# Two-layer sparse graph block on one core: hub slots fetched as runs of words, later record scatters, nine early gathers, two lists later

## The chip, the core and the metric

The kernel runs on one core of one Trainium2 chip. The metric is the device time in microseconds of one execution. A core has a matrix engine (TensorE, PE in the profile), three vector-like engines (VectorE or DVE, ScalarE or ACT, GpSimd or POOL), a sync engine (SP), and 16 DMA engines that move data between HBM and on-chip memory (SBUF). Each engine runs its own instruction queue in order; semaphores tie the queues together. PE writes into PSUM banks of 128 partitions x 512 words. Transfers that are issued by SP have fixed addresses; gathers and scatters by a list of row numbers are issued by POOL.

## The reference

x has 2708 rows of 1024 words; adj is a 2708 x 2708 matrix of zeros and ones, so sparse that a row has a handful of neighbours. All is float32. Two layers, each followed by a residual and a layer norm:

```python
q = x @ W_q.T + b_q;  k = x @ W_k.T + b_k;  v = x @ W_v.T + b_v
z = (q @ k.T) / sqrt(1024) * adj
z = where(z == 0, -10000, z)
x = layernorm(x + relu(softmax(z) @ v))          # layer 0: attention over neighbours
x = layernorm(x + adj @ (x @ weight) + bias)     # layer 1: sum over neighbours
```

## The kernel before

The kernel does not form the 2708 x 2708 scores. It uses the sparsity: M = W_q.T W_k once, y = x M, and the score of row n and neighbour m is the dot product of row n of y with row m of x. The attention output is the softmax-weighted sum r of the neighbours' rows of x, then turned by W_v.T. Rows without neighbours get the mean of all x. Rows are handled in 22 blocks of 128, sorted by degree so that each block has a fixed number of neighbour slots, `SLOTS`. Blocks 0 to 7 (`FAMILY` = 8) form the first family, blocks 8 to 21 the second; each family is sorted for itself.

**The stages, in order of time.**

1. The weights are loaded and transposed (to about 30 us).
2. M is computed on PE (`product_of_m`, to about 131 us). Behind its products DVE makes the neighbour lists: `list_columns` searches the six column ranges of one block of adj with `max_index` (L236) and leaves up to 24 column numbers per row in `keys`; `count_columns` lets ACT count the ones and loads the next block of adj. `EARLY` lists are spread over the products of M; the rest are put between the products of the y pairs by the table `between`. After list 9 the first family is sorted (`sort_begin(0)`, `sort_end(0)`).
3. y of blocks 0 to 7, in four pairs by a product scheme with fewer multiplications (`y_pair`, `pair_products`, L299); PE does them between 131 and 244 us. ACT or DVE empties the banks (`add`, L319 and L321). Behind the first pair the first family's records (neighbour numbers, row, degree; 28 words per row) are scattered into `tab_d` in sorted order and loaded back as `tabs`. `deal_hub` is a generator; each `next(deal)` emits its next part.
4. y of blocks 8 to 19, 21 and 20 one at a time (`y_block`, L379; `y_last`, L430; 244 to 466 us), each 32 matmuls of 512 columns. Beside each block the jobs of attention run: for the blocks 6, 5, 4, 3, 2, 2, 1, 1, hub, hub, 0, 0, 0 (blocks with many slots come in pieces of `PIECE` = 6). A job copies the constant y_bc into a tile on ACT (L472, L474), lets POOL add the gathered row of y onto it (`yg` or `xr`, L463), gathers one row of x per slot (`g`, L479, nine tiles in turn, `G1`), scores them on DVE (L1006), makes the softmax, and sums them on DVE (L1063, L1140) into `r`.
5. The attention products of block pairs and the first norm (466 to 756 us).
6. The second layer (756 to 1083 us): gathers of the normed rows, sums, products, norm.

**The hub.** The 32 rows of the highest degrees (`HUB`) have more neighbours than a record holds. Their rows of adj are cut into four quarters (`G` = 4), one per partition, and each quarter's neighbours (up to `HUB_KEYS` = 80) are drawn on DVE and stored as a list of `KW` = 96 words in DRAM, `keys_d`; the 16 words behind the 80 are zeros. The lists of all quarters lie behind one another. `place` holds at which dealt slot each list begins. The neighbours are dealt to 128 partitions of `HUB_SLOTS` = 11 slots each; a hub row gets as many partitions as it needs, and `row` says which hub row a partition works for. In the kernel before, the address of each slot is worked out on its own: eleven rows of DVE over all 128 lists (`at`, L592), and eleven gathers of one word per partition (`found`, in `gather_at`, L463), dealt out over four steps of the generator behind y blocks 11 to 14. From `found` come `valid_h` (L624), `less_h` and `tab_h`, the row numbers of the hub's gathers.

**What sets the order.** The queues are in order. POOL's queue holds the gathers, the scatters and a few table loads; a gather waits for its tile (its last reader on DVE) and for the landing of the POOL transfer eight before it. ACT's queue holds the bank copies and the copies of y_bc. The program order on each engine comes from a scheduler that takes instructions by priority; `tc.high_priority(URGENT)` puts an instruction ahead. `follow(later, earlier)` adds a wait by hand, most often for the last matmul of an earlier block, `products[-1]` or `products[-2]`, so that a queue doesn't stand still for something that is far off. In the main loop (L1363 to 1376) each y step runs `next(deal)`, `records_out` for the second family (two scatters a step into `tab_d`, L699, at blocks 10 to 16, and behind the last the load of the tables, L709), `records_back(1)` at block 19 (the copy into `degs`, L735, waits for block 18's products), and then the block's own products.

Pools give tiles their place in SBUF. A new tile on the place of a released pool waits for that pool's last users. `hub`, `work`, `g0` and `sums` are opened when the pools of the lists and y pairs (`lists`, `la`, `yb`) are released.

Of the kernel before, what the change touches and what calls it, by code (L numbers as in the profile page):

```python
# [9 lines left out]
F32 = mybir.dt.float32  # L10
BF16 = mybir.dt.bfloat16
I32 = mybir.dt.int32
# [4 lines left out]
ALU = mybir.AluOpType  # L17
# [4 lines left out]
P = 128  # L22
# [5 lines left out]
HUB_SLOTS = 11  # L28
HUB_KEYS = 80
FAMILY = 8  # L30

# [7 lines left out]
CLASSES = list(range(1, 14)) + [15, 17, 20, 24]  # L39
EARLY = 14  # L40
G1 = 9
# [40 lines left out]
def sparse_part(ctx, tc, x, xT, adj, wqT, wkT, wvT, bq, bk, bv, w1, b1, out):  # L82
# [28 lines left out]
    with es:  # L111
# [389 lines left out]
        def deal_hub():  # L501
# [39 lines left out]
            for i in range(0, HUB_KEYS, 8):  # L541
                nc.vector.max(keys[:, i:i + 8], a0)
                if i + 8 < HUB_KEYS:
# [41 lines left out]

            step = small("step", P)
            nc.vector.memset(step[:, 0:1], 0.0)
            nc.vector.scalar_tensor_tensor(step[:, 1:], place[:, :P - 1], float(KW), place[:, 1:], op0=ALU.add,
                                           op1=ALU.subtract)
            at = small("at", HUB_SLOTS)  # L590
            for j in range(HUB_SLOTS):
                nc.vector.scalar_tensor_tensor(junk, place, q[:, j:j + 1], step, op0=ALU.is_le, op1=ALU.mult,  # L592
                                               accum_out=at[:, j:j + 1])
            nc.vector.tensor_add(at, at, q)
            nc.vector.tensor_scalar_min(at, at, float(P * KW - 1))
            at_i = const.tile([P, HUB_SLOTS], I32, name="at_i")
            nc.vector.tensor_copy(at_i, at)

            row = small("row")
# [4 lines left out]
            nc.vector.tensor_copy(row_i, row)  # L604
            nc.vector.tensor_scalar(to_h, num, row, None, op0=ALU.is_equal)
            yield
            tr = p_tr.tile([P, 4, P], F32, name="tr")
# [11 lines left out]
            found = const.tile([P, HUB_SLOTS], F32, name="found")  # L619
            for j in range(HUB_SLOTS):  # L620
                gather_at(keys_d[:, :], at_i[:, j:j + 1], P, found[:, j:j + 1], behind=products[-1])
                if j % 3 == 2 or j == HUB_SLOTS - 1:
                    yield
            follow(nc.vector.tensor_scalar(valid_h, found, 0.0, None, op0=ALU.is_gt), products[-2])  # L624
            nc.vector.scalar_tensor_tensor(found, valid_h, -float(N + 1), found, op0=ALU.mult, op1=ALU.add)
# [218 lines left out]
        for b in range(0, FAMILY, 2):  # L844
            first = len(began)
            for k in range(min(3, NB - done)):
                if k:
                    between[first + 2 * k] = [lambda put: list_columns()]
                else:
                    list_columns()  # L850
                done += 1
                between[first + 2 * k + 1] = [count_columns]
            if b == 4:
                between[first + 4] = [lambda put: next(deal)]
            if b == 6:
# [20 lines left out]

        hp = es.enter_context(tc.tile_pool(name="hub", bufs=1, reuse_waits="tile"))
        wp = es.enter_context(tc.tile_pool(name="work", bufs=2, reuse_waits="tile"))
        gp = es.enter_context(tc.tile_pool(name="g0", bufs=G1, reuse_waits="tile"))
        rp = es.enter_context(tc.tile_pool(name="sums", bufs=RB, reuse_waits="tile"))  # L880
# [11 lines left out]
        def gather(src, b, word, n):  # L892
            return gather_slot(src, tabs[:n, b, word:word + 1], n, g_tile())

# [5 lines left out]
        def y_tile():  # L900

            filled[0] += 1
            if left_y and filled[0] % 4 in (3, 0):
                return wp.tile([P, D], F32, name="xr", bufs=2)
            return wp.tile([P, D], F32, name="yg")

# [162 lines left out]
        def r_tile(b):  # L1069

            if b in FIRST:
                return wp.tile([P, D], F32, name="r", tag="t")
            ring.append(b)
            return rp.tile([P, D], F32, name="r")
# [19 lines left out]
        def finish0(b, po, xr):  # L1094
            n = rows[b]
            t = (xb_pools[0] if b == last[-1] else wp).tile([P, D], F32, name="t", bufs=2)
            for h in range(NH):
# [90 lines left out]
        def project_pair(pair, A, S):  # L1188
            ts = [(xb_pools[0] if k else wp).tile([P, D], F32, name="t", bufs=2) for k in range(2)]
            bias = halves_of(bias_bc)  # L1190

            def whole(k, h, acc, what):
                add(halves_of(ts[k])[h], acc, what)

            pair_products(A, S, wv_q, wv_t, [bias, bias], [halves_of(t) for t in ts], whole, pair in (pairs[0], pairs[-1]))
            return ts
# [137 lines left out]
        for i, (kind, b) in enumerate(steps):  # L1334
# [29 lines left out]
            if kind == "y":  # L1364
                if FAMILY + 1 <= b < FAMILY + 7:
                    next(deal)
                if 2 <= b - FAMILY < 9:
                    records_out(*later_records, 2 * (b - FAMILY - 2), 2 * (b - FAMILY - 2) + 2, products[-2])
                if b == FAMILY + 11:
# [98 lines left out]
        def work1(unit, A, S, xrs):  # L1468

            ts = [wp.tile([P, D], F32, name="t", tag="t" if k % 2 == 0 else "yg") for k, _ in enumerate(unit)]  # L1470
            sums = [[stat.tile([P, 1], F32, name=f"sm{h}", bufs=6) for h in range(NH)] for _ in unit]
# [365 lines left out]
```

## Time and profile before

| what | us |
|---|---|
| six runs | 1089.21, 1091.35, 1085.18, 1079.99, 1079.20, 1075.07 |
| their median | 1082.58 |
| the profiled execution, its own time | 1084.41 |
| its span in the profile | 1082.7 |
| PE busy in the span | 963.5 (89%) |
| DVE busy | 834.7 (77%) |
| POOL busy | 562.1 (52%) |
| ACT busy | 410.2 (38%) |
| mean of one x gather on POOL (L479, 84 of them) | 1.341 |
| mean of one score on DVE (L1006) | 1.22 |
| one search of a list on DVE (L236, 132 of them), mean | 0.627 |
| granted clock of PE, mean | 0.957 |

How to read it: "us busy" of an engine is the time in which it executed; waits are the time in which an engine stood, put down to the instruction or transfer that ended the wait. `yo L319 <- PE` would mean a copy that waits for a product. Of a transfer the trace has the time of its issue on the engine's queue (what POOL is busy with) and the time when it lands. Line numbers are those of the kernel before, and in the changed kernel they are up to ten higher from the hub's part on. The windows by stage matter more than the sums, since the stages have different limits.

### The profile page before, as it was taken

How to read it: one execution, taken by the hardware profiler on the slowest of the kernel's cores; microseconds unless marked ns; L12 is line 12 of the kernel's file. 1: busy time of each engine (PE TensorE's matmuls, PEld its weight loads, DVE VectorE, ACT ScalarE, POOL GpSimd, SP SyncE). 2: the span in 40 equal slices, each digit the busy share in tenths (PEclk: the TensorE clock that was granted, in tenths of full speed). 3: DMA queues.
4: the chain of work that ended last, by engine and by line, in shares of the span. 5: the costliest groups of instructions: out<-in, count | busy, mean ns of one | idle time of the engine just before them, and what ended most of it. 6: DMA issues, size and time to landing. Idle time of an engine off the chain costs nothing.

```text
span 1082.7 us, 10444 instructions
## 1 busy us (share of the span) xinstructions
PE 963.5 (89%) x2697; PEld 450.9 (42%) x2697; DVE 834.7 (77%) x2045; ACT 410.2 (38%) x917; POOL 562.1 (52%) x454
## 2 busy tenths in 40 slices
PE   7999869999989589789999979897499999989894
PEld 6444324444434233335544434443244444435341
DVE  7999999926676778874999789677469877869632
ACT  4454445534433223414443434331312443351621
POOL 0441452305787574441766653554387777768420
PEclk9999899999999898899999999999699999999998
DMA  9567775648869766363468864669488789987741
GB/s 349 181 203 247 217 236 153 204 139 252 267 177 260 227 208 211 96 190 96 131 189 241 255 179 156 225 233 314 178 248 270 224 267 300 321 245 208 216 115 42
DMA packets 103293, 229.21 MB, mean 212 GB/s; under 512 B 19902, under 2 KB 47302, under 8 KB 103224
## 3 DMA queue, kind: packets, MB, share of 16 engines
q0 software_dynamic: 51376, 159.04, 48.3%
q1 hardware_dynamic: 51848, 69.41, 19.9%
q8 instruction: 23, 0.38, 0.1%
q14 instruction: 46, 0.38, 0.1%
HBM read 218.08 MB, written 33.64 MB: 232 GB/s over the span
## 4 chain that ended last, share of the span: by engine, by line
PE 23%; DVE 22%; issue 21%; DMA 17%; POOL 13%; ACT 1%; SPq 1%; POOLq 0%; another core or an unknown queue 0%; DVEq 0%; ACTq 0%
PE po L299 18%; POOL g L479 5%; DVE at_a L236 5%; DMA g<-in_x_dram,tabs 4%; DVE junkv L1006 3%; DVE r L1063 3%; DMA xr<-x_d,tabs 3%; PE po L379 2%; DMA yg<-y_d,tabs 2%; POOL xr L463 2%; POOL g L463 2%; DMA g<-x_d,tabs 1%; DMA wq_i<-in_wqT_dram 1%; DVE t L321 1%; DMA g<-in_x_dram,tab_h 1%
## 5 line engine op out<-in xcount | busy, mean ns | idle before, releaser
L379 PE MATMUL po<-m,xt 128*128 128x512 f32 x416 | 187.6, 612 | 22.2 <-ACT yo L319 22.2
L299 PE MATMUL po<-t,s_all 128*128 128x512 f32 x320 | 147.1, 603 | 14.9 <-DVE t L321 6.9
L479 POOL DMA_INDIRECT g<-in_x_dram,tabs x84 | 112.7, 1341 | 44.6 <-issue 17.7
L379 PEld LDWEIGHTS po<-m,xt 128*128 128x128 f32 x416 | 80.8, 196 | 126.6 <-issue 98.9
L1006 DVE SCALAR_TENSOR_TENSOR junkv<-yg,g 128x1024 uint8<-128x1024 f32 x69 | 84.2, 1221 | 41.3 <-DMA g<-in_x_dram,tabs 25.7
L1438 DVE SCALAR_TENSOR_TENSOR r<-g,valid,r 128x1024 f32<-128x1024 f32 x77 | 98.1, 1280 | 15.4 <-DMA g<-x_d,tabs 10.5
L299 PEld LDWEIGHTS po<-t,s_all 128*128 128x128 f32 x320 | 60.1, 192 | 97.4 <-issue 71.2
L299 PE MATMUL po<-wv,s_all 128*128 128x512 f32 x160 | 76.7, 624 | 13.1 <-DVE t L321 10.8
L479 POOL DMA_INDIRECT g<-x_d,tabs x66 | 75.3, 1141 | 24.5 <-issue 17.4
L968 ACT ACTIVATE junks<-t,lnm 128x1024 uint8<-128x1024 f32 (+1 forms) x40 | 45.9, 1147 | 105.2 <-DVE lnm L966 102.6
L1063 DVE SCALAR_TENSOR_TENSOR r<-g,pr,r 128x1024 f32<-128x1024 f32 x64 | 81.5, 1279 | 2.0 <-ACT r L1061 1.6
L236 DVE FIND_INDEX8 at_a<-ones,a 128x8 uint16<-128x83 f32 (+3 forms) x132 | 82.5, 627 | 0.0
L299 PE MATMUL po<-w,rT 128*128 128x512 f32 x160 | 74.3, 606 | 2.4 <-DVE t L1475 2.4
L299 PE MATMUL po<-t,rT 128*128 128x512 f32 x160 | 73.8, 603 | 1.9 <-DVE t L321 1.4
L252 ACT ACTIVATE junk<-a 128x2756 uint8<-128x2756 uint32 (+1 forms) x22 | 55.0, 2501 | 50.2 <-PE po L299 16.8
L299 PE MATMUL po<-w,s_all 128*128 128x512 f32 x160 | 72.3, 592 | 0.0
L926 ACT COPY rT<-tr 128x512 f32<-128x512 f32 x76 | 41.4, 587 | 77.7 <-PE tr L925 63.5
L299 PE MATMUL po<-wv,rT 128*128 128x512 f32 x160 | 70.6, 592 | 0.0
L981 ACT ACTIVATE t<-t,nmr,rstd 128x1024 f32<-128x1024 f32 (+1 forms) x40 | 49.1, 1239 | 52.7 <-DVE nmr L980 34.0
L452 ACT ACTIVATE junka<-xt 128x128 f32<-128x128 f32 x168 | 51.7, 307 | 39.0 <-PE po L299 30.4
L1006 DVE SCALAR_TENSOR_TENSOR junkv<-xr,g 128x1024 uint8<-128x1024 f32 x37 | 45.3, 1224 | 25.6 <-DMA g<-in_x_dram,tabs 11.0
L463 POOL DMA_INDIRECT xr<-in_x_dram,tabs x22 | 29.5, 1339 | 62.1 <-DVE t L1204 34.1
(408 smaller groups left out, 1732.9 us busy)
## 6 DMA issues: line engine op xcount, KB each, us to landing
xt<-in_xT_dram SPq DMA_DIRECT2D x21, 512.0 KB
y_d<-yo SPq DMA_DIRECT2D x21, 512.0 KB
a<-in_adj_dram SPq DMA_DIRECT2D x21, 413.5 KB
a<-in_adj_dram SPq DMA_DIRECT2D x21, 338.5 KB
a<-in_adj_dram SPq DMA_DIRECT2D x21, 263.5 KB
wq_i<-in_wqT_dram SPq DMA_DIRECT2D x8, 512.0 KB
wk_i<-in_wkT_dram SPq DMA_DIRECT2D x8, 512.0 KB
wv<-in_wvT_dram SPq DMA_DIRECT2D x16, 256.0 KB
```

Of the source, the lines that this page charges most:

```text
L236: nc.vector.max_index(at[:n, i], ones[:n, :8], a[:n, cuts[i] + 8 * i:cuts[i + 1] + 8 * i + 8])
L252: put = nc.scalar.activation(junk[:n], loaded[b][:n, :AW].bitcast(U32), AF.Sign, accum_out=cnt[:n, b:b + 1])
L299: put = nc.tensor.matmul(acc, a[:, k], w[:, k], start=start and k == 0, stop=stop and k == DC // 2 - 1, skip_group_check=True)
L379: put = nc.tensor.matmul(po, xts[b][:, c, :], m_q[c // 4][h][:, c % 4], start=(c == 0), stop=(c == DC - 1))
L452: put = nc.scalar.activation(junka[:, :xt.shape[2]], xt[:, c, :], AF.Copy, accum_out=xs[:, c, b:b + 1])
L463: put = nc.gpsimd.indirect_dma_start(out=dst[:n], out_offset=None, in_=src, in_offset=bass.IndirectOffsetOnAxis(ap=at, axis=0), compute_op=op)
L479: nc.gpsimd.indirect_dma_start(out=dst[:n], out_offset=None, in_=src, in_offset=bass.IndirectOffsetOnAxis(ap=at, axis=0), bounds_check=N - ...
L968: nc.scalar.activation(junks[:n], t[:n], AF.Square, bias=nm[:n], accum_out=vs[:n])
L981: applied.append(nc.scalar.activation(t[:n], t[:n], AF.Identity, bias=nmr[:n], scale=rstd[:n]))
L1006: nc.vector.scalar_tensor_tensor(junkv[:n], yg[:n], scale, xg[:n], op0=ALU.mult, op1=ALU.mult, accum_out=s)
L1063: nc.vector.scalar_tensor_tensor(r[:n], xg[j][:n], pr[:n, j:j + 1], r[:n], op0=ALU.mult, op1=ALU.add)
L1438: put = nc.vector.scalar_tensor_tensor(r[:n], xg[:n], ok[:n, j:j + 1], r[:n], op0=ALU.mult, op1=ALU.add)
```

## The change

Four parts, one diff.

- `EARLY` is 12 rather than 14: two lists are made behind the y pairs and not behind M. The pairs get 3, 4, 3 lists rather than 3, 3, 2. The hub's step in the third pair is moved two half products on.
- The hub's words are fetched as runs. Since the slots of one partition are consecutive words of at most four lists, a partition now reads a run of `RUN` = 12 words at one address per quarter, 4 gathers instead of 11. The address is clipped to the range from 11 words before the list to 81 in it, so that slots that belong to another quarter fall on zeros; one reduction over the four runs adds them. The generator ends at block 12 instead of block 14.
- The second family's 14 scatters go three a step at blocks 14 to 18 rather than two a step at blocks 10 to 16. The load of the tables follows the last, at block 18 instead of 16. `records_back(1)` stays at block 19.
- The first nine x gathers (those that fill the nine `g` tiles for the first time) have the priority `URGENT`. The `g0` pool moves ahead of `work`, and the tiles `yg`, `t` and the `r` of the blocks in `FIRST` move to a pool `worka` of their own ahead of both, so all of these lie on other memory than before.

In the order of the changed program POOL issues all nine early x gathers ahead of the first gather of y; before, four of them stood ahead of it. From the attention pairs on (stage 5) the order on every engine is as before.

```diff
--- before.py
+++ after.py
@@ -27,6 +27,7 @@
 HUB = 32
 HUB_SLOTS = 11
 HUB_KEYS = 80
+RUN = 12
 FAMILY = 8
 
 
@@ -37,7 +38,7 @@
 KEYS = 24
 RANGES = 6
 CLASSES = list(range(1, 14)) + [15, 17, 20, 24]
-EARLY = 14
+EARLY = 12
 G1 = 9
 RB = 5
 REC = 28
@@ -583,19 +584,6 @@
             nc.vector.tensor_scalar(full, n_r, 1.0, None, op0=ALU.is_lt)
             nc.vector.tensor_max(bad, bad, full)
 
-            step = small("step", P)
-            nc.vector.memset(step[:, 0:1], 0.0)
-            nc.vector.scalar_tensor_tensor(step[:, 1:], place[:, :P - 1], float(KW), place[:, 1:], op0=ALU.add,
-                                           op1=ALU.subtract)
-            at = small("at", HUB_SLOTS)
-            for j in range(HUB_SLOTS):
-                nc.vector.scalar_tensor_tensor(junk, place, q[:, j:j + 1], step, op0=ALU.is_le, op1=ALU.mult,
-                                               accum_out=at[:, j:j + 1])
-            nc.vector.tensor_add(at, at, q)
-            nc.vector.tensor_scalar_min(at, at, float(P * KW - 1))
-            at_i = const.tile([P, HUB_SLOTS], I32, name="at_i")
-            nc.vector.tensor_copy(at_i, at)
-
             row = small("row")
             nc.vector.scalar_tensor_tensor(junk[:, :HUB], place[:, 0::G], q[:, 0:1], ones[:, :HUB], op0=ALU.is_le,
                                            op1=ALU.mult, accum_out=row)
@@ -603,6 +591,18 @@
             row_i = const.tile([P, 1], I32, name="row_i")
             nc.vector.tensor_copy(row_i, row)
             nc.vector.tensor_scalar(to_h, num, row, None, op0=ALU.is_equal)
+            at = small("at", G)
+            for g in range(G):
+                nc.vector.scalar_tensor_tensor(junk[:, :HUB], to_h, 1.0, place[:, g::G], op0=ALU.mult, op1=ALU.mult,
+                                               accum_out=at[:, g:g + 1])
+            nc.vector.tensor_scalar(at, at, -1.0, q[:, 0:1], op0=ALU.mult, op1=ALU.add)
+            nc.vector.tensor_scalar(at, at, float(HUB_KEYS + 1), -float(HUB_SLOTS), op0=ALU.min, op1=ALU.max)
+            nc.vector.scalar_tensor_tensor(at, num[:, :G], float(KW), at, op0=ALU.mult, op1=ALU.add)
+            far_row = small("far_row")
+            nc.vector.tensor_scalar_mul(far_row, row, float(G * KW))
+            nc.vector.tensor_scalar(at, at, far_row, None, op0=ALU.add)
+            at_i = const.tile([P, G], I32, name="at_i")
+            nc.vector.tensor_copy(at_i, at)
             yield
             tr = p_tr.tile([P, 4, P], F32, name="tr")
             nc.tensor.transpose(tr[:, 0, :], row.to_broadcast([P, P]), ident)
@@ -617,11 +617,16 @@
             yield
             gather_at(tab_ds[0][:, :], row_i, P, rec_h, behind=products[-1])
             found = const.tile([P, HUB_SLOTS], F32, name="found")
-            for j in range(HUB_SLOTS):
-                gather_at(keys_d[:, :], at_i[:, j:j + 1], P, found[:, j:j + 1], behind=products[-1])
-                if j % 3 == 2 or j == HUB_SLOTS - 1:
+            found_g = const.tile([P, G, RUN], F32, name="found_g")
+            runs = keys_d.rearrange("n e -> e n")
+            for g in range(G):
+                follow(nc.gpsimd.indirect_dma_start(out=found_g[:, g, :], out_offset=None, in_=runs, in_offset=(
+                    bass.IndirectOffsetOnAxis(ap=at_i[:, g:g + 1], axis=1))), products[-1])
+                if g % 2:
                     yield
-            follow(nc.vector.tensor_scalar(valid_h, found, 0.0, None, op0=ALU.is_gt), products[-2])
+            put = nc.vector.tensor_reduce(found, found_g[:, :, :HUB_SLOTS].rearrange("p g j -> p j g"), AX.X, ALU.add)
+            follow(put, products[-2])
+            nc.vector.tensor_scalar(valid_h, found, 0.0, None, op0=ALU.is_gt)
             nc.vector.scalar_tensor_tensor(found, valid_h, -float(N + 1), found, op0=ALU.mult, op1=ALU.add)
             nc.vector.tensor_scalar_add(tab_h, found, float(N))
             far_from(valid_h, less_h)
@@ -843,7 +848,7 @@
             count_columns(began[-1])
         for b in range(0, FAMILY, 2):
             first = len(began)
-            for k in range(min(3, NB - done)):
+            for k in range(min(4 if b == 2 else 3, NB - done)):
                 if k:
                     between[first + 2 * k] = [lambda put: list_columns()]
                 else:
@@ -851,7 +856,7 @@
                 done += 1
                 between[first + 2 * k + 1] = [count_columns]
             if b == 4:
-                between[first + 4] = [lambda put: next(deal)]
+                between[first + 6] = [lambda put: next(deal)]
             if b == 6:
                 between[first + 5] = [lambda put: next(deal)]
             y_pair(b)
@@ -875,8 +880,9 @@
 
 
         hp = es.enter_context(tc.tile_pool(name="hub", bufs=1, reuse_waits="tile"))
+        wa = es.enter_context(tc.tile_pool(name="worka", bufs=2, reuse_waits="tile"))
+        gp = es.enter_context(tc.tile_pool(name="g0", bufs=G1, reuse_waits="tile"))
         wp = es.enter_context(tc.tile_pool(name="work", bufs=2, reuse_waits="tile"))
-        gp = es.enter_context(tc.tile_pool(name="g0", bufs=G1, reuse_waits="tile"))
         rp = es.enter_context(tc.tile_pool(name="sums", bufs=RB, reuse_waits="tile"))
         left_y, filled = NB - FAMILY, [0, 0]
         bias_bc = hp.tile([P, D], F32, name="bias_bc", tag="bias")
@@ -890,7 +896,11 @@
             return gp.tile([P, D], F32, name="g", tag=f"g{filled[1] % G1}", bufs=1)
 
         def gather(src, b, word, n):
-            return gather_slot(src, tabs[:n, b, word:word + 1], n, g_tile())
+            g = g_tile()
+            if filled[1] > G1:
+                return gather_slot(src, tabs[:n, b, word:word + 1], n, g)
+            with tc.high_priority(URGENT):
+                return gather_slot(src, tabs[:n, b, word:word + 1], n, g)
 
         def gather_x(src, b, k):
 
@@ -902,7 +912,7 @@
             filled[0] += 1
             if left_y and filled[0] % 4 in (3, 0):
                 return wp.tile([P, D], F32, name="xr", bufs=2)
-            return wp.tile([P, D], F32, name="yg")
+            return wa.tile([P, D], F32, name="yg")
 
         def gather_y(b):
             return gather_onto(b, y_bc, y_ds[b >= FAMILY][:, :], tabs[:rows[b], b, OFF:OFF + 1], rows[b],
@@ -1069,7 +1079,7 @@
         def r_tile(b):
 
             if b in FIRST:
-                return wp.tile([P, D], F32, name="r", tag="t")
+                return wa.tile([P, D], F32, name="r", tag="t")
             ring.append(b)
             return rp.tile([P, D], F32, name="r")
 
@@ -1093,7 +1103,7 @@
 
         def finish0(b, po, xr):
             n = rows[b]
-            t = (xb_pools[0] if b == last[-1] else wp).tile([P, D], F32, name="t", bufs=2)
+            t = (xb_pools[0] if b == last[-1] else wa).tile([P, D], F32, name="t", bufs=2)
             for h in range(NH):
                 hs = slice(h * HALF, (h + 1) * HALF)
                 with tc.high_priority(URGENT):
@@ -1186,7 +1196,7 @@
             return [wm_pool.tile([P, DC // 2, HALF], F32, name=f"t{k}", tag=f"m{k - 2}") for k in (2, 3, 4)]
 
         def project_pair(pair, A, S):
-            ts = [(xb_pools[0] if k else wp).tile([P, D], F32, name="t", bufs=2) for k in range(2)]
+            ts = [(xb_pools[0] if k else wa).tile([P, D], F32, name="t", bufs=2) for k in range(2)]
             bias = halves_of(bias_bc)
 
             def whole(k, h, acc, what):
@@ -1362,10 +1372,11 @@
             if not left_y:
                 turn(i)
             if kind == "y":
-                if FAMILY + 1 <= b < FAMILY + 7:
+                if FAMILY + 1 <= b < FAMILY + 5:
                     next(deal)
-                if 2 <= b - FAMILY < 9:
-                    records_out(*later_records, 2 * (b - FAMILY - 2), 2 * (b - FAMILY - 2) + 2, products[-2])
+                if 6 <= b - FAMILY < 11:
+                    k0 = 3 * (b - FAMILY - 6)
+                    records_out(*later_records, k0, min(k0 + 3, NB - FAMILY), products[-2])
                 if b == FAMILY + 11:
                     records_back(1)
                     nc.sync.dma_start(out=bias_bc, in_=bv.to_broadcast([P, D]))
@@ -1467,7 +1478,7 @@
 
         def work1(unit, A, S, xrs):
 
-            ts = [wp.tile([P, D], F32, name="t", tag="t" if k % 2 == 0 else "yg") for k, _ in enumerate(unit)]
+            ts = [wa.tile([P, D], F32, name="t", tag="t" if k % 2 == 0 else "yg") for k, _ in enumerate(unit)]
             sums = [[stat.tile([P, 1], F32, name=f"sm{h}", bufs=6) for h in range(NH)] for _ in unit]
 
             def whole(k, h, acc, what):
```

## The prediction

> **What bounds the kernel now.** I read the windows by stage first, because the shares over the whole span (PE 89%, DVE 77%, POOL 52%) mix stages. Columns: window, its length, then busy us with the number of instructions of each engine, the granted clock, the DMA share, GB/s.
>
> ```profile
> 45.00:164.00 119.00, 102.93 (x234) 44.41 (x232) 118.87 (x455) 54.85 (x77) 50.94 (x39) 0.94 0.76 227
> 164.00:244.00 80.00, 79.98 (x195) 36.60 (x196) 56.21 (x219) 40.29 (x125) 15.33 (x14) 0.98 0.52 163
> 244.00:300.00 56.00, 56.00 (x133) 24.83 (x132) 39.41 (x96) 25.59 (x86) 38.81 (x28) 1.00 0.86 255
> 300.00:350.00 50.00, 45.45 (x102) 19.52 (x101) 36.60 (x59) 19.12 (x72) 38.88 (x29) 0.97 0.78 223
> 350.00:400.00 50.00, 37.05 (x82) 15.92 (x81) 34.21 (x57) 11.79 (x47) 32.93 (x26) 0.90 0.72 222
> ```
>
> From 45 to 164 us (M and the first y pair) DVE is full, 118.87 of 119, and PE has 16.1 us of holes: the neighbour lists set the pace. From 164 to 244 (the other y pairs) PE is full and DVE has 24 us free. From 300 on PE has holes again, while neither DVE (36.60 of 50) nor POOL is full. So I asked PE's waits who makes them (us in total, times, longest):
>
> ```profile
> PE po L379 <- ACT yo L319: 22.2, 6, 10.9
> PE po L299 <- DVE yo L321: 10.5, 1, 10.5
> PE po L430 <- ACT yo L319: 7.7, 1, 7.7
> ```
>
> The 10.5 stands in the first y pair (it ends at 164.02), where DVE still has lists ahead of the addition that frees the bank. The 22.2 and 7.7 stand in the y blocks: PE waits for a bank that ACT has not emptied. ACT is not slow. Its largest idle stretch there, 18.38 us before 367.94, is a copy of y_bc into a tile that DVE's score line L1006 still reads, with the bank's copy behind it. So DVE is late, and its own waits in the windows 244 to 300, 300 to 350 and 350 to 400 say why:
>
> ```profile
> DVE junkv L1006 <- DMA g<-in_x_dram,tabs: 11.0, 5, 4.3
> DVE junkv L1006 <- DMA yg<-y_d,tabs: 5.2, 1, 5.2
> ...
> DVE junkv L1006 <- DMA g<-in_x_dram,tabs: 13.1, 7, 5.6
> ...
> DVE junkv L1006 <- DMA g<-in_x_dram,tabs: 4.1, 1, 4.1
> DVE valid_h L624 <- DMA found<-keys_d,at_i: 3.5, 1, 3.5
> ```
>
> With the 5.2, 36.9 us up to 362 us are waits for gathers. Those come from POOL's queue, which the timeline shows nearly without a hole from 249.80 to 358 (start, us, then the idle time before):
>
> ```profile
> 322.77 1.57 POOL L463 DMA_INDIRECT found<-keys_d,at_i  x1 [0.30 <-issue]
> 324.65 2.01 POOL L463 DMA_INDIRECT found<-keys_d,at_i  x1 [0.30 <-issue]
> 326.96 0.95 POOL L463 DMA_INDIRECT found<-keys_d,at_i  x1 [0.30 <-issue]
> 328.21 1.01 POOL L479 DMA_INDIRECT g<-in_x_dram,tabs  x1 [0.30 <-issue]
> 329.53 1.01 POOL L479 DMA_INDIRECT g<-in_x_dram,tabs  x1 [0.30 <-issue]
> 335.45 1.80 POOL L479 DMA_INDIRECT g<-in_x_dram,tabs  x1 [2.32 <-DVE nm L1033]
> ```
>
> Three fetches of hub words stand ahead of the gather of 328.21, which lands 4.44 us later, and DVE stands 5.59 us until 332.75. The chain in the y blocks is therefore POOL issue, landing, DVE score, ACT copy, bank, PE.
>
> **Part 1, two lists later.** A list is six searches (0.23+0.39+0.55+0.70+0.86+1.02 = 3.75 us) and about 0.85 us of small rows, so two are 9.2 us of DVE work, moved from the full stage into the pairs. Summing the DVE rows in program order up to the second block's addition of the first pair gives 149.6 us before and 142.4 in the changed order: 7.2 less, since part of the moved work still stands ahead of it. The additions of M come 6.8 to 7.0 earlier by the same sum. What is late next is PE itself: 16.1 us of holes are there, so 7 fits. The moved work goes under 164 to 244, where DVE has 24 us free. The other additions of the pairs then come 0.1 to 4 us before PE wants them; without that cover part of the 7 goes. I take **7.0**, bounds 0 and 9.2.
>
> **Part 2, the hub's words.** Removed: 11 issues, 285.12 to 347.53, busy 15.8 plus 0.30 between each, 19.1 us of POOL. Added: 4 issues. No row fetches a run of 12 words per partition; the nearest are one word (found, mean 1434 ns), 28 words (rec_h, 0.97 us) and 1024 words (g, 1304 ns). The length of the run does not show in the issue, so I take 1.74 with the pause, 7.0 in all: 12.1 us less. The upper end is each word costing what a found issue does, 12 x 1.43 + 0.3 = 17.5 us, 70 in all. On DVE, eleven at rows (0.35 and 0.08, 4.7 us) become four smaller ones, and one small reduction is added, bounded by 0 and the 0.33 of the 128x176 reduction; both lie in or beside DVE's wait for yg until 256.05 and I cost them at 0. If that cover went, they would bring up to 3 us. The reduction waits for the four transfers, as valid_h did (3.5 us), and the scores are behind it on DVE: 0 to 3.5.
>
> **Part 3, the scatters.** Ten of the 14 stand ahead of the hub's first gather (361.90); afterwards six do. Four times 1155 + 300 ns is 5.8 us less there. They return where POOL has room (the gathers with tab show 27.3 us of idle before them). Each now waits for PE's block two back, in triples, with the x gathers behind them on POOL. The table's load follows the last: I put it near 390 us, against DVE's copy of degs, at 442.65 before and near 422 after. So 30 us of cover; if that is gone, DVE stands at degs for the excess.
>
> **Part 4, nine early gathers.** Five x gathers of 253.57 to 262.34 (6.7 us busy, 8.2 with pauses) move ahead of the first yg and under the pairs, where POOL is busy 15.33 of 80 and the DMA share is 0.52. They also take 2.6 MB out of the window at 0.86. What is late next for DVE is yg: its 5.2 us stay. Against this, the queue now reaches rec_h, which waits for the end of y block 9, sooner: I count 5.5 us in which POOL stands and a gather stands behind it.
>
> **The sum.** POOL's relief is 12.1 + 5.8 + 8.2 = 26.1, less 5.5, 20.6 us. Not all of it reaches DVE, by a row that the timeline shows: while DVE stands (326.96 to 332.75) four issues take 0.99 to 1.01 us, and the next, beside DVE's score, 1.80. A filled DVE hole thus makes issues longer: some 0.77 issues fit in one us (1.0 and 0.3), each 0.7 longer, 0.54 us per us. X = 20.6 - 0.54 X gives **13.4** us. The Trainium skill's page "SBUF — State Buffer", section "SBUF: two separate sides", speaks against the change here: a vector operation with two SBUF operands and GpSimd hold one port pair in turn, and the loser stands for the whole instruction. If every issue paid that in full (0.99 to 2.05 in these rows), each us of filled hole would cost 0.8, and X would be 11.4.
>
> 7.0 + 13.4 = 20.4 us. The y blocks can give at most PE's holes there, some 36 us, and about 5 for blocks slowed by a granted clock of 0.88 to 0.90. Behind the stage the programs are alike and PE is near full (490 to 540: 50.00 of 50), so I carry the gain to the end. The profiled execution took 1084.41 us (span 1082.7 and 1.7 around it), close to the median of 1082.58. Forecast: 1084.4 - 20.4 = **1064 us**.
>
> **Rivals.**
> - *The relief is larger.* No lengthening, no stand at rec_h, clock recovered: 7 + 26.1 + 5 = 38 us, 1046. For: the lines at 322.77. Against: the lengthened issues are visible. 0.09.
> - *Only the lists pay.* The triples that wait for PE hold the gathers as long as the fetches did, or DVE's tight additions keep some of the 7: 1077, up to 1084 if they keep it all. For: POOL now runs close behind PE in order. Against: a POOL that waits for a PE without holes costs nothing. 0.18.
> - *Slower, by one mechanism:* the four run fetches are written out word by word, 1536 pieces each where a found has 128. At 17.5 us each POOL holds the queue 70 us near 270, 51 more than before instead of 12 less; the relief of 20.6 becomes -42, and DVE stands about that long: 1084 - 7 + 42 = 1119. It decides from where the loss eats the 7: 4 issues at 7.0 + 20.6 + 7 over 4, about 8.7 us each. For: no row has such a fetch. Against: 28 and 1024 words in a row issue as one does. 0.14.
> - *The change does not do what it says:* the nine gathers stay behind yg because their tiles wait for memory still used by lists or y sums, and rec_h stands; then 7 + (17.9 - 5.5)/1.54 - 8 for moved work that collides, some 7 us, which falls in the list case's range. 0.04.
>
> **How the numbers follow.** The forecast case (1048 to 1073) has 0.55. Together 0.55, 0.09, 0.18, 0.14 and 0.04. Faster by over 1% (below 1073.6; 1% is about what a measurement of this kernel can tell from no change): 0.55 + 0.09 + 0.06 of the list cases = 0.70. Slower by over 1%: 0.14 and 0.02 for a late table. Within: 0.14. The range leaves out the slow case and the lower end of the large relief: 1042 to 1088.
>
> **What would show it.** The end of the last y pair near 237 instead of 244; nine x gathers ahead of the first yg; four found_g issues of 1 to 2 us; DVE's waits for x gathers before 362 down from 28 us to about 15; the end of y block 20 near 446 instead of 466 and PE's L379 waits at half; degs without a wait. Wrong would make it: a found_g issue over 9 us, DVE standing at degs or at the reduction, POOL idle behind PE at L699 with DVE idle behind it, or a shortened y stage followed by a larger PE wait after 490.

## The result and the profile after

The changed kernel takes 1084.46 us (median of 39 runs) against 1080.63 us (81 runs of the kernel before): a ratio of 1.0038, 95% interval 1.0024 to 1.0053. It is some 4 us slower, within the 1% that I called no change. A gain of 20.4 us, to 1064, was forecast, and none of it came. The profiled execution has a span of 1087.2 us.

The windows by stage of the changed kernel (columns as for the kernel before):

```profile
45.00:164.00 119.00, 104.36 (x241) 46.13 (x240) 114.78 (x416) 49.88 (x75) 42.63 (x37) 0.94 0.68 203
164.00:244.00 80.00, 72.79 (x171) 32.21 (x170) 66.14 (x250) 42.82 (x120) 21.89 (x21) 0.96 0.64 213
244.00:300.00 56.00, 56.00 (x137) 25.40 (x136) 32.34 (x82) 27.95 (x95) 29.55 (x20) 1.00 0.85 218
300.00:350.00 50.00, 50.00 (x118) 22.18 (x117) 35.67 (x63) 16.27 (x62) 27.69 (x20) 1.00 0.81 252
350.00:400.00 50.00, 41.57 (x89) 17.86 (x88) 39.36 (x59) 16.59 (x64) 33.21 (x25) 0.91 0.61 190
```

Two things stand out. PE now has holes where it was full, in the y pairs: 72.79 of 80 after 79.98. And POOL is far less busy from 244 to 350: 57.2 us after 77.7. For the second, one stretch in both kernels, 250 to 362, where the hub's words used to be fetched. Before:

```profile
250.00:362.00 112.00, 106.25 (x244) 46.16 (x242) 74.59 (x132) 40.45 (x148) 84.44 (x64) 0.98 0.82 245
```

After:

```profile
250.00:362.00 112.00, 105.94 (x244) 46.61 (x243) 74.68 (x143) 46.67 (x170) 64.34 (x44) 0.98 0.81 228
```

POOL (fifth figure after the length) has 20.1 us less to do, and DVE (third) did the same 74.6 us of work in the same time. The relief came as it was counted, and bought DVE nothing: counted from PE's first product of the y blocks (243.9 us before, 248.9 now), the sixtieth of DVE's score rows begins after 194.4 us before and after 194.1 in the changed kernel. POOL's timeline of the changed kernel shows what took the place of the fetches:

```profile
317.84 1.93 POOL L480 DMA_INDIRECT g<-in_x_dram,tabs  x1 [4.21 <-ACT r L1071]
320.07 1.00 POOL L480 DMA_INDIRECT g<-in_x_dram,tabs  x1 [0.30 <-issue]
321.38 1.01 POOL L480 DMA_INDIRECT g<-in_x_dram,tabs  x1 [0.30 <-issue]
322.70 0.99 POOL L480 DMA_INDIRECT g<-in_x_dram,tabs  x1 [0.30 <-issue]
328.14 1.80 POOL L480 DMA_INDIRECT g<-in_x_dram,tabs  x1 [4.45 <-DVE scores L1023]
...
350.07 0.99 POOL L480 DMA_INDIRECT g<-in_x_dram,tabs  x1 [4.20 <-DVE r L1073]
354.98 1.92 POOL L480 DMA_INDIRECT g<-in_x_dram,tabs  x1 [3.92 <-DVE scores L1023]
```

In the bracket is POOL's idle time before the gather and what ended it. POOL no longer runs without a hole: it stands 4 us at a time until DVE or ACT has read an older row. A gather writes one of nine tiles, and a tile comes free only when its row has been summed (L1071, L1073). The brackets name `scores` twice, but this is a small row beside the sum: the sum ends at 327.87 and at 354.71, each time 0.27 us before POOL goes on. DVE's waits from 250 to 440 accordingly did not shrink (in us, times, longest):

```profile
DVE junkv L1016 <- DMA g<-in_x_dram,tabs: 26.3, 16, 4.1
DVE alike L609 <- PE tr L608: 9.9, 1, 9.9
DVE junkv L1016 <- DMA g<-in_x_dram,tab_h: 8.8, 7, 3.7
DVE junkv L1016 <- DMA g<-in_x_dram,tab: 4.8, 3, 2.2
```

The three waits for gathers of x are 39.9 us in all; the same three rows of the kernel before are 28.2, 7.7 and 5.4, 41.3 us. The 9.9 is new. Before its first score DVE now stands for a transpose of the hub's step on PE (`alike`), which the changed order puts ahead of that score, where it stood 5.2 us for yg before. The first score begins 14.6 us after PE's first product of the y blocks, and began after 12.2.

The other change is in M and the pairs. PE's timeline from 100 to 250 us:

```profile
126.99 0.87 PE L675 MATMUL mm<-hot,lower 128*128 128x152 f32 x2 [11.67 <-DVE hot L669]
160.30 3.70 PE L300 MATMUL po<-y_t,xt 128*128 128x512 f32 x8 [2.97 <-DVE yo L322]
190.50 6.47 PE L300 MATMUL po<-y_t,xt 128*128 128x512 f32 x8 [5.90 <-DVE yo L322]
219.76 3.70 PE L300 MATMUL po<-y_t,xt 128*128 128x512 f32 x8 [1.31 <-DVE yo L322]
```

The wait of 10.5 us in the first pair is down to 2.97, as foretold. But a new one of 11.67 stands in M, where PE's sort matmul waits for DVE's input, and 5.90 in the second pair. The four rows are 21.9 us; the waits of the kernel before in the same stretch are 0.2, 4.0, 0.2, 1.2 and 10.5, 16.1. The y blocks start at 248.9 and not 243.9.

### The profile page after: what moved, and what is told of

The parts are those of the page before. It is cut to its first block, busy times and chain, and to the rows that moved or that the text cites. A ratio compares the mean times of both kernels' runs of the same rounds, so it can differ in the third digit from the quotient of the medians.

```text
span 1087.2 us, 10401 instructions
## 1 busy us (share of the span) xinstructions
PE 965.2 (89%) x2697; PEld 453.5 (42%) x2697; DVE 840.3 (77%) x2033; ACT 411.1 (38%) x917; POOL 548.9 (50%) x447
## 4 chain that ended last, share of the span: by engine, by line
PE 24%; DVE 24%; issue 21%; DMA 15%; POOL 12%; ACT 3%; POOLq 0%; another core or an unknown queue 0%; DVEq 0%; ACTq 0%
PE po L300 18%; DMA g<-in_x_dram,tabs 5%; POOL g L480 5%; DVE at_a L237 5%; DVE junkv L1016 3%; DVE r L1073 3%; POOL xr L464 2%; DMA yg<-y_d,tabs 2%; PE po L380 2%; POOL g L464 2%; DMA g<-x_d,tabs 2%; DVE r L1449 1%; DMA g<-in_x_dram,tab 1%; POOL tab_d L704 1%; PE tr L272 1%
## 5 line engine op out<-in xcount | busy, mean ns | idle before, releaser
L300 PE MATMUL po<-t,s_all 128*128 128x512 f32 x320 | 149.3, 610 | 21.9 <-DVE xr L322 12.6
L480 POOL DMA_INDIRECT g<-in_x_dram,tabs x84 | 113.1, 1346 | 88.8 <-issue 16.2
L480 POOL DMA_INDIRECT g<-x_d,tabs x66 | 77.9, 1181 | 25.5 <-issue 17.4
L1073 DVE SCALAR_TENSOR_TENSOR r<-g,pr,r 128x1024 f32<-128x1024 f32 x64 | 81.8, 1280 | 4.0 <-ACT r L1071 3.7
L935 PE MATMUL tr<-ident,r 128*128 128x128 f32 x304 | 41.2, 285 | 23.0 <-DVE r L1446 14.3
```

The lines of the kernel that those rows point to most:

```text
L300: put = nc.tensor.matmul(acc, a[:, k], w[:, k], start=start and k == 0, stop=stop and k == DC // 2 - 1, skip_group_check=True)
L480: nc.gpsimd.indirect_dma_start(out=dst[:n], out_offset=None, in_=src, in_offset=bass.IndirectOffsetOnAxis(ap=at, axis=0), bounds_check=N - ...
L1073: nc.vector.scalar_tensor_tensor(r[:n], xg[j][:n], pr[:n, j:j + 1], r[:n], op0=ALU.mult, op1=ALU.add)
```

## The experiments

Each is compared with runs of the kernel before on the same chip; the ratio is to those. The medians of the kernel before lie between 1077.36 and 1078.78 us there and at 1080.63 over the 81 runs, so rows are compared by their ratios. u_hub and lists11 have four runs, tiles8 five.

| run | what | median us | ratio, 95% interval |
|---|---|---|---|
| u_lists | change, 14 lists | 1077.48 | 0.9991 (0.9965 to 1.0016) |
| u_hub | change, 11 one-word gathers | 1085.01 | 1.0079 (1.0056 to 1.0101) |
| u_early | change, old order of early gathers | 1083.54 | 1.0063 (1.0025 to 1.0101) |
| u_scat | change, early scatters | 1084.33 | 1.0071 (1.0039 to 1.0103) |
| tiles8 | change, 8 gather tiles | 1097.24 | 1.0165 (1.0113 to 1.0216) |
| nobias9 | change, bias terms left out | 1084.61 | 1.0052 (1.0017 to 1.0087) |
| nobias10 | the same, 10 tiles | 1072.69 | 0.9948 (0.9911 to 0.9985) |
| pace | change, 12 lists at the pace of 14 | 1079.73 | 1.0026 (1.0000 to 1.0052) |
| before10 | before, 10 tiles | 1082.03 | 1.0021 (0.9982 to 1.0061) |
| before11 | before, 11 tiles | 1077.73 | 1.0003 (0.9969 to 1.0037) |
| lists10 | u_lists, 10 tiles | 1069.47 | 0.9908 (0.9876 to 0.9940) |
| lists11 | u_lists, 11 tiles | 1063.16 | 0.9886 (0.9814 to 0.9959) |
| lists11b | the same again | 1066.58 | 0.9895 (0.9842 to 0.9948) |
| pace10 | pace, 10 tiles | 1074.62 | 0.9986 (0.9957 to 1.0014) |
| l11_hub | lists11, 11 one-word gathers | 1074.54 | 0.9960 (0.9929 to 0.9991) |
| l11_early | lists11, old order of early gathers | 1065.86 | 0.9876 (0.9838 to 0.9914) |
| l11_scat | lists11, early scatters | 1067.39 | 0.9892 (0.9851 to 0.9933) |
| pace334 | see below | 4783.59 | 4.4385 (4.4207 to 4.4562) |

**One part undone at a time.** u_lists:

```diff
-EARLY = 12
+EARLY = 14
-            for k in range(min(4 if b == 2 else 3, NB - done)):
+            for k in range(min(3, NB - done)):
-                between[first + 6] = [lambda put: next(deal)]
+                between[first + 4] = [lambda put: next(deal)]
```

> The changed kernel with fourteen lists behind M again (the first part undone, the other three kept). Theory 1, the two late lists turned into new waits (in the changed kernel PE waits 11.7 us for the sort's input at 115 to 127 us and 5.9 us for a bank in the second pair, and the y blocks start 4.9 us later): the sort wait goes, the 10.5 us wait in the first pair comes back, the y blocks start near 244, and the time is 4 to 6 us below the changed kernel's, 1078 to 1081. Theory 2, the step of the prediction holds and the lists are worth a gain that something later hides: the time is the same as the changed kernel's or up to 7 us above it.

u_hub takes back the address rows and the eleven gathers of the kernel before:

> The changed kernel with the eleven one-word gathers and their address rows in place of the four runs (the second part undone). Theory 1, in the changed kernel POOL no longer sets the pace of the y blocks, the nine gather tiles do (POOL stands for the release of a tile): 12 us more of POOL work fill POOL's holes and the time stays within 4 us of the changed kernel's. Theory 2, POOL's issues still set the pace, as the prediction had it: 12 us more of POOL are 8 to 12 us more of time, 1092 to 1096.

u_early takes back the priority, the pool `worka` and the pools' order:

> The changed kernel without the priority of the first nine x gathers and with the pools and tiles where they were before (the fourth part undone). Theory 1, the tiles set the pace: gathers that come early only fill the nine tiles earlier, the first scores wait for the gather of y in both, and the time stays within 4 us of the changed kernel's. Theory 2, POOL sets the pace: five gathers, 8 us, come back into the full stretch and the time grows by 5 to 8 us.

u_scat takes back the two scatters a step from block 10 on:

> The changed kernel with the second family's scatters two a step from block 10 on and the tables' load at block 16 (the third part undone). Theory 1, the tiles set the pace: within 3 us of the changed kernel's. Theory 2, POOL sets the pace: 4 to 6 us slower, since four scatters come back ahead of the hub's gathers. A third way, the triples that wait for PE at blocks 14 to 18 hold gathers up: 3 to 8 us faster.

The lists cost 0.47% (1.0038 to 0.9991), 5 us. Undoing one of the others leaves the kernel 0.2 to 0.4% above the changed one, 2 to 4 us, near what theory 1 has and short of theory 2's 8 to 12 for u_hub; u_early's and u_scat's intervals overlap that of the changed kernel, u_hub's, from four runs, begins just above it. Taken together without the lists, the three parts, which take 20 us from POOL's fullest stretch, give a kernel that equals the one before. Where the gain goes is seen in PE's timeline of u_lists:

```profile
352.41 37.36 PE L380 MATMUL po<-m,xt 128*128 128x512 f32 x80 [6.53 <-ACT yo L320]
391.30 7.13 PE L380 MATMUL po<-m,xt 128*128 128x512 f32 x16 [1.53 <-ACT junka L453]
407.93 9.06 PE L380 MATMUL po<-m,xt 128*128 128x512 f32 x16 [9.50 <-ACT pr L1143]
...
441.49 0.58 PE L1168 MATMUL mm<-den,tops 128*128 128x1 f32 x2 [4.86 <-DVE den L1164]
464.73 1.11 PE L935 MATMUL tr<-ident,r 128*128 128x128 f32 x4 [5.51 <-ACT rT L936]
```

Matched matmul by matmul with the kernel before, PE is 16.9 us ahead at 392. Then it waits 9.50 for a bank, 4.86 for the hub's denominator on DVE and 5.51 at the first turned sum, and at 465 it is 2.9 ahead. PE ran ahead and stood until DVE had caught up: DVE had not become earlier (its sixtieth score begins 193.7 us after the start of the y blocks, 194.4 before).

**More and fewer tiles.** tiles8 sets `G1 = 8`:

> The changed kernel with eight gather tiles in turn instead of nine. Theory 1, the nine tiles pace the y blocks (a gather waits until DVE has summed the row nine gathers back, then lands 4.4 to 6 us later): one tile less makes DVE stand longer at its score line, 8 to 20 us slower than the changed kernel, 1091 to 1104. Theory 2, POOL's issue times or PE pace it: within 3 us of the changed kernel.

A tenth tile does not fit beside the nine, so two runs leave the bias terms out and differ in the number of tiles alone:

```diff
-        bias_bc = hp.tile([P, D], F32, name="bias_bc", tag="bias")
+        bias_bc = y_bc
-        bias1 = hp.tile([P, D], F32, name="bias1", tag="bias")
-        nc.sync.dma_start(out=bias1, in_=b1.to_broadcast([P, D]))
+        bias1 = y_bc
```

> The changed kernel with nine gather tiles and without the loads of the two bias rows: the constant y_bc is added in their place, which leaves the two bias terms out of the result and frees 4 KB per partition. It is the base for the run with ten tiles. Both theories: within 2 us of the changed kernel, since the two loads are 0.5 MB each and no wait in the profile is put down to them.

> As the run with nine tiles and the bias terms left out, but with ten gather tiles in the freed memory. Theory 1, the tiles pace the y blocks: 4 to 15 us faster than with nine, DVE's waits for gathers of x shorter. Theory 2, POOL or PE pace them: within 2 us of the run with nine.

One tile less costs 1.3% (1.0038 to 1.0165, 14 us), one more gives 1.0% (1.0052 to 0.9948, 12 us). The number of tiles paces the changed kernel. Did it pace the one before? The tenth and eleventh tile can be had with the whole result kept, because two of the five tiles for sums are not taken until blocks 1 and 0 are summed (before10 and lists10 use only the last):

```diff
+        turns, sums_taken = [f"g{k}" for k in range(G1)] + [f"r{k}" for k in range(3, RB)], [0]
 ...
-            return gp.tile([P, D], F32, name="g", tag=f"g{filled[1] % G1}", bufs=1)
+            tag = turns.pop(0)
+            while tag[0] == "r" and sums_taken[0] > int(tag[1:]):
+                tag = turns.pop(0)
+            turns.append(tag)
+            return (gp if tag[0] == "g" else rp).tile([P, D], F32, name="g", tag=tag, bufs=1)
```

> The kernel before with a tenth gather tile during the first thirteen jobs: the last of the five tiles for sums serves as a gather tile until block 0's sum takes it. Everything else as before, the result whole. Theory 1, the tiles paced the y blocks already before the change: 5 to 12 us faster than before, 1067 to 1074. Theory 2, before the change POOL's issues paced them (as the prediction had it) and the tiles only do so since: within 3 us of before.

> The kernel before with a tenth and an eleventh gather tile (the sums' tiles of blocks 0 and 1 until those need them). Theory 1, two limits lie close together, POOL's issues and the tiles, and before the change POOL's came first: within 4 us of before. Theory 2, the tiles were the only limit and the tenth failed for another reason: 6 to 15 us faster than before, like the changed kernel with eleven.

> The changed kernel with fourteen lists behind M (three parts of the change kept) and the tenth gather tile in the same way. Theory 1, the tiles pace the y blocks and POOL's relief counts once they do so less: 8 to 14 us faster than the same kernel with nine tiles (1077.5), 1063 to 1070, and below the kernel before with ten tiles by 2 to 6 us. Theory 2, the three kept parts bring nothing in any case: the same as the kernel before with ten tiles, within 2 us.

> As the run with fourteen lists and ten tiles, but with eleven: the fourth sum's tile serves as a gather tile too until block 1's sum takes it. Theory 1: a further 1 to 5 us, less than the tenth brought, since DVE's idle time shrinks and the eleventh is there for half of the jobs only. Theory 2, the gain of the tenth tile came from something else than the wait for a free tile: no change, within 1 us.

> The changed kernel with fourteen lists and eleven tiles again, with more rounds: 1061 to 1067, 1.1 to 1.6% below before.

In the kernel before, more tiles give nothing (1.0021 and 1.0003); in the one without the lists' part they give 0.8% and 1.0%. So neither is the limit alone. POOL's relief alone: 0.9991. Two tiles alone: 1.0003. Both: 0.9886 and 0.9895, 11 to 12 us. DVE's waits from 250 to 440 point the same way. before11:

```profile
DVE junkv L1011 <- DMA g<-in_x_dram,tabs: 23.8, 9, 9.8
DVE junkv L1011 <- DMA g<-in_x_dram,tab_h: 10.7, 6, 3.6
DVE junkv L1011 <- DMA g<-in_x_dram,tab: 5.2, 6, 2.6
```

lists11b:

```profile
DVE junkv L1021 <- DMA g<-in_x_dram,tabs: 14.4, 9, 3.5
DVE alike L609 <- PE tr L608: 9.9, 1, 9.9
DVE junkv L1021 <- DMA g<-in_x_dram,tab: 8.4, 6, 3.0
DVE junkv L1021 <- DMA g<-in_x_dram,tab_h: 6.9, 5, 2.5
```

For gathers of x, 39.7 us with the tiles alone, against 41.3 without either; 29.7 with both. These are single executions, and the sums follow the times only roughly: they are 37.3 in lists10 and in u_hub, whose ratios are 0.9908 and 1.0079. The start of the sixtieth score is another measure: 187.1 us after the start of the y blocks in before11, 180.7 in lists11b, 194.4 before. The profiled execution of before11, 1071.24 us, was faster than its median of 1077.73. So a small gain of the tiles alone is not ruled out by the trace; the ten runs show none, within 0.4%.

**Which part of the relief counts once the tiles are there.** The same three undoings, beside eleven tiles:

> The changed kernel with fourteen lists and eleven gather tiles, but the eleven one-word gathers of the hub in place of the four runs. With eleven tiles and all three POOL parts it was 1063.2. If POOL's issues count once tiles are free, 12 us more of them cost 5 to 10 us: 1068 to 1073. If the tiles alone made the gain: within 3 us.

> The changed kernel with fourteen lists and eleven gather tiles, but the nine early gathers in their old order and the pools where they were. If POOL's issues count once tiles are free, 8 us of them come back into the full stretch: 3 to 7 us slower than 1063.2. If not: within 3 us.

> The changed kernel with fourteen lists and eleven gather tiles, but the scatters two a step from block 10. If POOL's issues count once tiles are free, four scatters (5.8 us) return ahead of the hub's gathers: 2 to 5 us slower than 1063.2. If not: within 3 us, or faster where the triples held the queue.

Of the three only the hub's words show an effect: 0.9960 against 0.9886 and 0.9895, 7 to 8 us, for the 12.1 us of POOL that they take. The interval touches those of lists11, lists11b and l11_scat at the edge and is clear of that of l11_early. DVE's three waits are back at 38.3 us in that run:

```profile
DVE junkv L1017 <- DMA g<-in_x_dram,tabs: 25.7, 9, 6.3
DVE junkv L1017 <- DMA g<-in_x_dram,tab: 7.9, 4, 4.3
DVE alike L610 <- PE tr L609: 7.1, 1, 7.1
DVE junkv L1017 <- DMA g<-in_x_dram,tab_h: 4.7, 4, 1.5
```

l11_hub also brings back the eleven address rows on DVE, 4.7 us before. They are not what costs: they go under the wait at `alike` (7.1 where lists11b has 9.9), and the first score begins 14.6 us after the start of the y blocks in both. The sixtieth begins after 190.2, and after 180.7 in lists11b. The early gathers and the scatters' places show no effect (0.9876, 0.9892).

**The lists.** pace changes one line, so that the ninth list comes behind product 18 again:

```diff
-            while done < EARLY * worked // (7 * DC // 2):
+            while done < min(EARLY, 14 * worked // (7 * DC // 2)):
```

> The changed kernel with its twelve lists made at the pace of fourteen (the ninth list behind product 18 of M, as before, not behind product 21), so that the sort of the first family gets its input in time. Theory 1: PE's wait of 11.7 us for the sort's input falls below 2 us, M ends 6 us earlier than in the changed kernel; the second pair's wait for a bank stays (four lists there), so the y blocks start 3 to 6 us earlier; but since DVE and not PE sets the end of the y blocks, the whole gains 2 to 5 us, 1077 to 1080. Theory 2, PE's start of the y blocks carries to the end: 6 to 10 us, 1072 to 1076.

> The changed kernel with its twelve lists at the pace of fourteen and the tenth gather tile. Theory 1: as with fourteen lists and ten tiles within 3 us, since the start of the y blocks differs by a few us only and DVE sets their end. Theory 2, with the tiles relieved PE's start of the y blocks counts: 3 to 6 us below it or above it by as much as the y blocks start earlier or later.

The 11.67 at the sort is gone (0.18), and the whole gains 0.12% against the changed kernel, with intervals that overlap. But the first pair's wait is back:

```profile
112.16 0.53 PE L675 MATMUL mm<-hot,lower 128*128 128x152 f32 x2 [0.18 <-DVE hot L669]
...
163.18 5.35 PE L300 MATMUL po<-y_t,xt 128*128 128x512 f32 x8 [11.29 <-DVE yo L322]
```

With twelve lists it is 11.29, with fourteen (u_lists) 10.53. At an equal pace, two lists fewer do not bring that addition forward at all: it begins at 162.46, and in u_lists at 162.29. In the changed kernel the wait was only smaller because PE had already lost 11.67. DVE's waits from 100 to 250 in pace say what took the place of the moved work:

```profile
DVE hub_i L533 <- DMA rec_r<-tab_d,r_i: 4.5, 1, 4.5
```

`hub_i` is made from the first record of the hub (`rec_r`), which POOL scatters, loads back and gathers. Up to the addition DVE works 152.4 us in pace and 157.0 in u_lists, 4.6 less, and it stands 4.48 at `hub_i`, which in pace lies ahead of the addition. The record does not come earlier because lists are fewer. With ten tiles twelve lists are again slower than fourteen, 1074.62 against 1069.47.

> Twelve lists at the pace of fourteen, three, three and four lists in the first three pairs, the hub's runs, the late scatters, the early gathers, and eleven tiles. Theory 1, the fourth list in the second pair was what was left of the first part's loss: the second pair's wait of 5.9 us goes, the y blocks start 3 to 8 us earlier than with fourteen lists, and the time is 2 to 6 us below that of fourteen lists with eleven tiles. Theory 2, DVE has no room for a further list anywhere in the pairs, since the first job's rows wait behind them: 2 to 6 us above it.

pace334 says nothing on that: the fourth list's place in the third pair is the one that the hub's step is written into, so one list was never made; the kernel found its lists incomplete and went through its dense path, 4783.59 us. So it stays open where a fourth list would be free, and what the moved work would be worth with `hub_i` behind the addition.

## Why the prediction was wrong

**The y blocks: the step "what is late next".** The sum turned 20.6 us of relief on POOL into 13.4 us on DVE, limited only by longer issues and by PE's holes. The relief is right: 20.1 us less POOL work from 250 to 362. The step to DVE failed, because the next limit was not asked for at the gather itself: a gather needs an issue slot and a free tile. In the profile of before, POOL's brackets in the stretch read 0.30 almost everywhere, which says that POOL was the later of the two, but not by how much. before10 and before11 show that POOL was indeed first, u_lists beside lists11 that the tiles were directly behind it, tiles8 and nobias10 that they pace the changed kernel. In the measure of the whole, the term of 13.4 was 1 us (u_lists, 0.9991, an interval from 4 us faster to 2 slower). The step on part 4, that yg's 5.2 us stay, failed too: the order of the changed program makes it 9.9 at `alike`. In the old order of the gathers (u_early) the first score begins after 11.9 us instead of 14.6; no difference in time can be told from the noise.

**The lists: the step "7.0".** The sum over DVE's rows ahead of one addition moved only that addition. What was left out is the sort: it needs nine lists, and with twelve spread over the same 28 products the ninth comes later, while its matmul keeps its place in PE's queue (11.67 us). The second thing left out is the hub's first record, for which DVE stood only 0.7 before:

```profile
DVE hub_i L533 <- DMA rec_r<-tab_d,r_i: 6.7, 1, 6.7
```

The records are scattered from 141.33 on instead of 136.93, and `rec_r` is issued at 164.63 instead of 163.14, 1.5 us later; the rest of the 6.7 is DVE arriving earlier and standing. The bank of the second pair is behind it on DVE, where the four lists are too: 5.90. So 7.0 gained was 5.0 lost at the start of the y blocks, and u_lists gives 5 us for the whole. pace shows that even the bare term was wrong: with the sort in time, 4.6 us less work on DVE became a wait of 4.48 for that record, and no us of the 7.0 came. PE's holes, which the prediction named as next, were not: the record was.

**Terms that held.** The four run fetches took 1.80, 0.94, 1.14 and 1.90 us of issue, 7.0 with pauses, as taken. So the slower rival, each word a piece of its own, did not happen, and needed over 8.7. All nine early gathers stand ahead of the first yg; degs has no wait. The triples of scatters, which the rival "only the lists pay" feared, hold nothing up: each of the 14 stands 0.30 on POOL, and u_scat and l11_scat are not faster. That rival's time, up to 1084, came out, but by chance, from other causes: the lists lost where it had them gain, and POOL's relief met the tiles.

**Terms that were off without deciding.** I counted 5.5 us of POOL standing at rec_h; it waited 0.30. PE's holes in the y blocks were put at some 36 us; from 244 to 466 PE is busy 192.1 of 222, so they were 29.9. Issues did not get longer on the whole, 1346 ns a gather of x (L480, all 84) after 1341; the change does not test the term, since DVE's holes were not filled. In lists11b 11.6 us of DVE's waits are gone; at 0.54 us each that would be 6.3 us, some 75 ns on each of the 84 (an estimate from these rows), and the mean is 1321. In lists10 it is 1369 and in l11_early 1391, so the single profiles scatter by as much, and no lengthening is shown. The term was read from one row. Beside the rows at 320 to 328 us (1.00, 1.01, 0.99, then 1.80), DVE sums without a break from 317.60 to 321.53, so the issue of 1.00 at 320.07 stood beside DVE's work as the 1.80 did: an issue beside DVE's work can be longer and need not be.

The rule of the Trainium skill's page "SBUF — State Buffer", section "SBUF: two separate sides", on the shared port has a condition that the prediction left out: a vector operation with two SBUF inputs takes the port only against a GpSimd operation that reads SBUF. No run here shows whether the issue of an indirect transfer is one. The rule agrees in direction with the 1.80 and not with the 1.00.

## What to carry to other kernels

A gather here starts when its queue has a slot and its buffer is free. Before pricing a relief on the one, ask when each buffer was last read: if the queue's waits would turn into waits for the buffer at once, the relief is worth nothing until buffers are added, and the buffers nothing without the relief (0.9991 and 1.0003 alone, 0.9886 together). One buffer less or more shows whether the buffers are the limit now (tiles8, nobias10). It does not show that they are the next limit, as before10 with its 1.0021 says: for that the relief and the buffers have to be changed together. When work is thinned out ahead of something that needs the nth piece, follow the nth piece, not the total; and when work is taken off a queue, ask which wait further down it was covering (here the one for the hub's record, 0.7 before and 4.5 in pace).

## What was not expected

Two tiles that lay idle, those for the sums of the last two jobs, together with the hub's fetches as runs and fourteen lists, make a kernel 1.1% faster than the one before (0.9886, 0.9895), with the whole result. And, as the prediction took it without a row to show it, an indirect gather of 12-word runs is issued in the time of a one-word gather (0.94 to 1.90 us against 0.95 to 2.01).
